# A graph network's prologue: one tied order for index look-up, one-hots and layer norm

## The chip, the cores and the metric

The kernel runs on one core of a Trainium2 chip. The metric is the device time of one execution in microseconds (us), the median of several runs on the same chip. Engines are named as in the profile: PE (TensorE, the matrix engine; PEld is its weight load), DVE (VectorE), ACT (ScalarE), POOL (GpSimd) and SP (SyncE). PE, DVE, ACT and POOL each work through their own instructions in the order in which the program lists them; semaphores tie them to each other.

## The reference

There are 6,250 nodes with 64 features and 206,250 directed edges (100,000 random pairs in both directions and a loop at each node), sorted by destination. Two residual layers follow each other:

```python
edge_index = jnp.stack([src, dst])
h = jnp.maximum(_layernorm(x, axis=-1), 0.0)
x = x + _L0_gnn_ref(h, edge_index, ...)   # two graph convolutions: sum over the edges, two dense layers each
h = jnp.maximum(_layernorm(x, axis=-1), 0.0)
x = x + _L1_gnn_ref(h, edge_index, ...)   # three dense layers per node, sum over the edges, three dense layers
```

All sums over edges use the same graph, so the kernel first turns the edge list into a matrix of edge counts and then multiplies by it.

## The kernel before

**Tiling.** The nodes are cut into 49 tiles of 128. The count matrix A is built tile by tile (index t): function `build` makes one-hot matrices on DVE (`there` L413, `high` L417, `low` L420), PE multiplies them into counts (L445; a block is 16 small products, and four blocks make a tile), and ACT copies each block out of PSUM into the tile `a` (L447). SP stores `a` to memory. While tile t is built, PE also does the first graph sum for tile t-1 (L588: 49 products with the normalized features `hp`), a quarter after each block. After the 49 tiles come two sweeps over the stored A (L754, L761), which this change does not touch.

**Index chain.** Tiles are handled in pairs; a batch b holds two pairs (batch 0 only one). For a batch, in this order: `search` (ACT L311 counts samples below a node; DVE L315 and L316 make a row number), `fetch_blocks` (POOL L324 gathers a block of 550 destinations per pair), `search_block` (ACT L335 counts in the block), `fetch_edges` (DVE L344 and L345 make offsets; POOL L349 gathers 128 windows of destinations and of sources, `d_win` and `s_win`), `slots` (eight kinds of DVE instruction, L372 to L388, that cut the indices into three fields), `cast` (ACT L394), `turn` (three PE transposes L402 into one bank, copied by ACT L404 into `lkw`), and then the one-hots. In the steady state each step of a later batch is put between the blocks of an earlier one, through the table `beside`, whose entries `between` runs after each block.

**Layer norm.** The features are normalized in seven chunks of seven tiles (XT = 7). `values(c)` calls `norm`: DVE mean (L238, L239), centred values `xm` (L241), ACT squares (L243), DVE sum of squares (L245), ACT root (L246), DVE reciprocal and scaling into `h` (L247, L248). Then `split` cuts `h` into three bf16 parts: ACT casts the first (L255), PE multiplies `h` by the identity and subtracts the parts already taken (L258, L260) into bank 0 and then bank 1 of a PSUM tile, and ACT copies each bank out (L261). The texts below call the L258 product into bank 0 the first product of a chunk and that into bank 1 the second. The PSUM pool `pcnt` has two tiles of two banks, shared by the splits and by the count blocks in program order. The tile `h` has two buffers, and so have the three one-hot tiles.

**Order.** The engine order comes from the tile framework's scheduler, except where `behind(op, other)` or `follow` adds a dependence without a semaphore between instructions of one engine. In the kernel before, the prologue's program order is: searches and block gathers of batches 0 and 1, `values` of chunks 0 and 1 around the gathers of batch 0, `slots` and `cast` of batch 0, gathers of batch 1, `turn` of batch 0, chunk 2, search of batch 2, chunk 3, search of batch 3, chunk 4, then the loop over tiles. Chunks 5 and 6 follow in the loop after tile 0's build. `slots`, `cast` and `turn` of batch 1 stand between the blocks of tile 0. The x chunks are loaded alternately from the SP queue (chunks 0, 2, 4, 6) and the ACT queue (1, 3, 5), behind the sample load `smp_i` on SP. Quoted with the function that the change rewrites most:

```python
    def values(t):
        h = work.tile([P, XT, D], FP, name="h")
        begun, centered, squared = norm(h, t, XT)
        if t <= XT:
            behind(begun, sampled)
            behind(begun, bounds)
            behind(squared, searched[0])
        if t == XT:
            behind(centered, searched[1])
        split(hp[:, t:t + XT], h)
```

Of the kernel before, what the change touches and what calls it, by code (L numbers as in the profile page):

```python
# [32 lines left out]
FP = mybir.dt.float32  # L33
I32 = mybir.dt.int32
I16 = mybir.dt.int16
# [5 lines left out]
OP = mybir.AluOpType  # L41
# [107 lines left out]
def load_x(nc, xs, x, engines):  # L149
    full = N // P  # L150
    nc.vector.memset(xs[:, full, :], 0.0)
    for i, t in enumerate(range(0, full, XT)):
        n = min(XT, full - t)
        engines[i % len(engines)].dma_start(xs[:, t:t + n, :], x[t * P:(t + n) * P].rearrange("(t p) d -> p t d", p=P))
    engines[0].dma_start(xs[:N - full * P, full, :], x[full * P:])


@with_exitstack
def fast(ctx: ExitStack, tc: tile.TileContext, x, src, dst, w, bad, out):
# [14 lines left out]
    def bank(name, dtype=FP):  # L174
        return pmix.tile([P, CH * 4 // mybir.dt.size(dtype)], dtype, tag="mix", name=name)


    root = const.tile([P, 1], FP, name="root")
    nc.scalar.activation(root, w.eps, AF.Sqrt)
# [1 line left out]
    with nc.allow_non_contiguous_dma(reason="samples"):  # L181
        nc.sync.dma_start(smp_i, dst.rearrange("(k c b) -> k c b", c=SP_COLS, b=BLK)[:, :, 0])
    xs = const.tile([P, NT, D], FP, name="xs")
    load_x(nc, xs, x, [nc.sync, nc.scalar])
    w.load(nc.sync)


# [9 lines left out]
    nc.vector.tensor_scalar(ident_a, w.ident, 1.0 / UNIT, None, op0=OP.mult)  # L197
# [9 lines left out]


    smp_f = once.tile([SP_ROWS, SP_COLS], FP, name="smp_f")
    nc.vector.tensor_copy(smp_f, smp_i)  # L210
    nc.vector.memset(smp_f[0:1, 0:1], -1.0)
    smp_d = once.tile([SP_ROWS, SP_COLS, SP_ROWS], FP, name="smp_d")
    shape = [SP_ROWS, SP_COLS, SP_ROWS]
# [20 lines left out]
    def norm(to, t, n):  # L234

        xt = xs[:, t:t + n, :]
        mean = work.tile([P, n], FP, name="mean", tag=f"mean{n}")
        begun = nc.vector.tensor_reduce(mean, xt, axis=AX.X, op=OP.add)  # L238
        nc.vector.tensor_scalar_mul(mean, mean, 1.0 / D)  # L239
        xm = work.tile([P, n, D], FP, name="xm", tag=f"xm{n}")  # L240
        centered = nc.vector.tensor_tensor(xm, xt, mean[:, :, None].to_broadcast([P, n, D]), op=OP.subtract)  # L241
        sq = work.tile([P, n, D], FP, name="sq", tag=f"sq{n}", bufs=1)
        squared = nc.scalar.activation(sq, xm, AF.Square)  # L243
        var = work.tile([P, n], FP, name="var", tag=f"var{n}")
        nc.vector.tensor_reduce(var, sq, axis=AX.X, op=OP.add)  # L245
        nc.scalar.activation(var, var, AF.Sqrt, bias=w.eps, scale=1.0 / D)  # L246
        nc.vector.reciprocal(var, var)  # L247
        nc.vector.scalar_tensor_tensor(to, xm, 0.0, var[:, :, None].to_broadcast([P, n, D]), op0=OP.max, op1=OP.mult)  # L248
        return begun, centered, squared

    def split(parts, h):

        parts = [parts[:, :, i * D:(i + 1) * D] for i in range(NP)]
        banks = pcnt.tile([P, 2, CH], FP, name="cnt")[:, :, :h.shape[1] * D]
        nc.scalar.copy(parts[0], h)  # L255
        for i in range(2):
            ps = banks[:, i].rearrange("p (t d) -> p t d", d=D)
            nc.tensor.matmul(ps, w.ident, h, start=True, stop=False)  # L258
            for k in range(i + 1):
                nc.tensor.matmul(ps, minus, parts[k], start=False, stop=(k == i))  # L260
            nc.scalar.copy(parts[i + 1], ps)  # L261
# [23 lines left out]
    counted, swept = {}, []  # L285

    def behind(op, other):

        tc.add_manual_dep(op.ins, other.ins.name,
                          mybir.DependencyInfo(mybir.DependencyClass.NoSync, mybir.DependencyReason.DATA),  # L290
                          reason="order on an engine")
        return op

    def follow(op, engine):

# [40 lines left out]
        follow(op, "ACT")  # L336
        return op

    def fetch_edges(b):

        if b >= len(BATCHES):
            return
        each, qs = tiles_of(b)
        nc.vector.scalar_tensor_tensor(off_f[:, qs], sign2[:, qs], -0.5, base[:, qs], op0=OP.mult, op1=OP.add)  # L344
# [10 lines left out]
    def slots(b):  # L355

        if b >= len(BATCHES):
            return
# [8 lines left out]

        def first(op):
            follow(op, "DVE")

        pair = temp("pair")
        first(nc.vector.tensor_scalar(pair, d, 1, PITCH // 2 - 1, op0=OP.logical_shift_right, op1=OP.bitwise_and))  # L372
# [2 lines left out]
        for i, q in enumerate(each):  # L375
# [12 lines left out]
        nc.vector.scalar_tensor_tensor(parts[:, :, 2, :].bitcast(I16), place, ONE_BITS, second,  # L388
                                       op0=OP.bitwise_or, op1=OP.bitwise_or)
        words[b] = word  # L390

    def cast(b):
# [3 lines left out]
    def turn(b, i):  # L396

        if b >= len(BATCHES):
            return
        ps = bank("ps_win", BF)  # L400
        for k in range(3):
            follow(nc.tensor.transpose(ps[:, k * P:(k + 1) * P], parts2[b % 2][:, i, k, :], identb), "PE")  # L402
        lkw = lkws[starts[b] + i] = wins.tile([P, 3, P], BF, name="lkw", bufs=5)
        nc.scalar.copy(lkw.rearrange("p a b -> p (a b)"), ps[:, :3 * P])  # L404

    def hot(lkw, g0, n):
# [6 lines left out]
        nc.vector.tensor_tensor(there, word2[:, None, :, :].to_broadcast(shape),  # L413
                                of(0)[:, :, None, :].to_broadcast(shape), op=OP.is_equal)
# [5 lines left out]
        counted["DVE"] = nc.vector.tensor_tensor(  # L420
            low.rearrange("p (g i) w -> p g i w", i=2), there.rearrange("p g w i -> p g i w"),
            of(2)[:, :, :, None].to_broadcast([P, n // 2, 2, W]), op=OP.mult)
        return low.bitcast(F8), high

    def store(t, a):
# [8 lines left out]
    def build(t, between):  # L434
# [1 line left out]
        a = amat.tile([P, H, G], I16, name="a", tag="a")  # L436
        lkw = lkws[t // 2]
        for g0, m in FIRST_HOTS if t == 0 else ((0, G),):
            low, high = hot(lkw, (t % 2) * G + g0, m)
            for k in range(g0, g0 + m, 2 * PG):  # L440
                ps = pcnt.tile([P, 2, CH], FP, name="cnt")
                for b in range(2):
# [68 lines left out]
    def values(t):  # L511
        h = work.tile([P, XT, D], FP, name="h")
        begun, centered, squared = norm(h, t, XT)
        if t <= XT:
            behind(begun, sampled)
            behind(begun, bounds)
            behind(squared, searched[0])
        if t == XT:
            behind(centered, searched[1])
        split(hp[:, t:t + XT], h)  # L520


    beside = {}
    for b in range(len(BATCHES)):
        step = BATCHES[b]

        def at(u, what, *args):
            beside.setdefault(8 * starts[b] + u * step // 2, []).append((what, args))

        at(0, slots, b + 1)  # L530
        at(4, cast, b + 1)
        for i in range(BATCHES[b + 1] if b + 1 < len(BATCHES) else 0):
            at(7 + 2 * i, turn, b + 1, i)
        if b > 0:
            at(6, search, b + 4)
            for i in range(BATCHES[b + 3] if b + 3 < len(BATCHES) else 0):
                at(10 + 2 * i, search_block, b + 3, i)
            at(13, fetch_edges, b + 3)
            at(14, fetch_blocks, b + 4)
# [10 lines left out]
    fetch_blocks(0)  # L550
    search(1)
    fetch_blocks(1)
    values(0)
    search_block(0, 0)
    fetch_edges(0)
    values(XT)
    slots(0)
    cast(0)
    for i in range(2):
        op = search_block(1, i)  # L560
    fetch_edges(1)
    turn(0, 0)
    values(2 * XT)
    search(2, op)
    fetch_blocks(2)
    values(3 * XT)
    search(3)
    fetch_blocks(3)
    values(4 * XT)
    for i in range(2):  # L570
        search_block(2, i)
    fetch_edges(2)

    r1, acc1 = {}, {}

# [31 lines left out]
    for t in range(NT + 1):  # L607
        last_total, total = total, FirstSum(t - 1, a) if t else None
        if t < NT:
# [7 lines left out]

            a = build(t, between)
            if t == 0:
                values(5 * XT)  # L620
                for i in range(2):
                    search_block(3, i)
                fetch_edges(3)
                values(6 * XT)
                search(4)
                fetch_blocks(4)
            if t == 1:
# [416 lines left out]
```

## Time and profile before

| what | value |
|---|---|
| median of 3 runs | 892.75 us (892.65 to 893.2) |
| profiled execution, its own time | 895.53 us |
| profiled execution, span of the trace | 893.7 us |
| busy in the span: PE, DVE, ACT, POOL | 96%, 71%, 63%, 14% |
| mean granted TensorE clock | 0.989 |
| PE busy from 61.1 to 120 us | 57.58 of 58.90 us |
| PE busy from 0 to 61.1 us | 38.46 of 61.10 us |

The span is what the trace covers; 1.8 us of the profiled execution lie around it. The last line adds the seven windows of the prologue (1.62 + 5.51 + 4.32 + 5.14 + 5.94 + 8.78 + 7.15). A timeline line gives the start in us, the time in us, engine, source line and operation, output and input, and the number of merged instructions; a bracket tells how long the engine was idle before it and who released it. Note that one product with fp32 operands is two instructions in the trace.

### The profile page before, as it was taken

How to read it: one execution, taken by the hardware profiler on the slowest of the kernel's cores; microseconds unless marked ns; L12 is line 12 of the kernel's file. 1: busy time of each engine (PE TensorE's matmuls, PEld its weight loads, DVE VectorE, ACT ScalarE, POOL GpSimd, SP SyncE). 2: the span in 40 equal slices, each digit the busy share in tenths (PEclk: the TensorE clock that was granted, in tenths of full speed). 3: DMA queues.
4: the chain of work that ended last, by engine and by line, in shares of the span. 5: the costliest groups of instructions: out<-in, count | busy, mean ns of one | idle time of the engine just before them, and what ended most of it. 6: DMA issues, size and time to landing. Idle time of an engine off the chain costs nothing.

```text
span 893.7 us, 19691 instructions
## 1 busy us (share of the span) xinstructions
PE 854.5 (96%) x8227; PEld 730.8 (82%) x8227; DVE 633.7 (71%) x908; ACT 566.0 (63%) x761; POOL 126.9 (14%) x86
## 2 busy tenths in 40 slices
PE   3789999999999999999999999999999999999996
PEld 1369999999999999978887878888889877777784
DVE  6889999999999999645545555554556676767662
ACT  5757776667776666645555555555546579777763
POOL 4535334354342200000000000000000000000000
PEclk9799999999999999999999999999999999999998
DMA  6335564455545534644444444444434677777771
GB/s 145 103 99 163 150 171 130 140 165 159 142 134 145 148 111 130 198 131 125 129 123 118 124 129 124 118 121 133 128 92 125 181 222 244 232 235 234 218 220 38
DMA packets 148326, 133.57 MB, mean 149 GB/s; under 512 B 29988, under 2 KB 110500, under 8 KB 148228
## 3 DMA queue, kind: packets, MB, share of 16 engines
q1 hardware_dynamic: 141784, 121.19, 46.5%
q0 software_dynamic: 3600, 10.32, 4.4%
q8 instruction: 66, 1.08, 0.5%
q10 hardware_dynamic: 2844, 0.72, 0.4%
q14 instruction: 32, 0.26, 0.1%
HBM read 91.25 MB, written 40.94 MB: 148 GB/s over the span
## 4 chain that ended last, share of the span: by engine, by line
PE 88%; ACT 4%; DMA 3%; DVE 2%; issue 2%; SPq 0%; POOL 0%; ACTq 0%; DVEq 0%
PE acc L761 43%; PE acc L588 23%; PE cnt L445 9%; PE ps_t L458 6%; PE ps_y L467 3%; ACT ar L754 2%; DMA a<-A 2%; PE ps_g L508 1%; PE cnt L258 1%; DMA xs<-in_x_dram 1%; ACT t L460 1%; ACT a L447 1%; PE acc L590 0%; DMA blk<-in_dst_dram,row 0%; PE ps_win L402 0%
## 5 line engine op out<-in xcount | busy, mean ns | idle before, releaser
L754 DVE CAST ar<-a 128x2048 fp32r<-128x2048 uint8 (+1 forms) x200 | 220.4, 1110 | 183.1 <-PE acc L761 158.4
L754 ACT CAST ar<-a 128x2048 fp32r<-128x2048 uint8 (+2 forms) x126 | 232.2, 1845 | 126.4 <-PE acc L761 108.6
L761 PE MATMUL acc<-ar,h2r 128*128 128x512 f32 (+2 forms) x1274 | 297.6, 388 | 0.0
L761 PEld LDWEIGHTS acc<-ar,h2r 128*128 128x128 f32 x1274 | 229.3, 188 | 49.8 <-issue 5.8
L588 PE MATMUL acc<-hp,a 128*128 128x193 bf16 x2401 | 237.1, 247 | 6.6 <-issue 5.8
L447 ACT ACTIVATE a<-cnt 128x784 int16<-128x784 f32 x196 | 160.8, 822 | 83.9 <-PE cnt L445 82.8
L588 PEld LDWEIGHTS <-a 128*128 128x128 fp8e4 x2401 | 196.4, 98 | 10.0 <-issue 7.8
L761 PE MATMUL acc<-ar,yr 128*128 128x512 f32 (+2 forms) x637 | 157.6, 399 | 0.0
L761 PEld LDWEIGHTS acc<-ar,yr 128*128 128x128 f32 x637 | 115.7, 188 | 32.5 <-issue 9.8
L445 PEld LDWEIGHTS <-low 128*128 128x128 fp8e4 x3136 | 107.6, 96 | 10.7 <-issue 10.4
L445 PE MATMUL cnt<-high,low 128*128 128x49 bf16 x3136 | 114.1, 186 | 1.8 <-ACT a L447 1.6
L420 DVE TENSOR_TENSOR low<-there,lkw 128x2048 int32<-128x2048 bf16 (+2 forms) x51 | 112.2, 2199 | 0.0
L417 DVE TENSOR_TENSOR high<-high,lkw 128x3136 bf16<-128x3136 bf16 (+2 forms) x51 | 87.9, 1723 | 19.5 <-PE cnt L445 18.7
L324 POOL DMA_INDIRECT blk<-in_dst_dram,row x25 | 48.0, 1918 | 99.3 <-DVE base L316 86.7
L413 DVE TENSOR_TENSOR there<-word,lkw 128x2048 bf16<-128x2048 bf16 (+2 forms) x51 | 59.1, 1177 | 0.9 <-ACT lkw L404 0.4
L349 POOL DMA_INDIRECT s_win<-in_src_dram,off x25 | 45.4, 1815 | 7.6 <-issue 7.6
L349 POOL DMA_INDIRECT d_win<-in_dst_dram,off x25 | 31.4, 1254 | 72.5 <-DVE off L345 64.9
L258 PE MATMUL cnt<-h,ident 128*128 128x448 f32 x28 | 19.6, 804 | 13.2 <-DVE h L248 9.1
L460 ACT ACTIVATE t<-ps_t,d 128x512 f32<-128x512 f32 (+2 forms) x26 | 17.3, 664 | 11.2 <-PE ps_t L458 11.1
L460 ACT ACTIVATE t<-ps_t,c 128x512 f32<-128x512 f32 (+1 forms) x26 | 17.1, 662 | 11.4 <-PE ps_t L458 11.4
L258 PEld LDWEIGHTS cnt<-h,ident 128*128 128x128 f32 x28 | 5.8, 252 | 19.6 <-issue 10.8
L335 ACT ACTIVATE junk<-blk,below_node 128x550 bf16<-128x550 int32 x25 | 18.7, 749 | 3.8 <-DMA blk<-in_dst_dram,row 3.8
(122 smaller groups left out, 598.2 us busy)
## 6 DMA issues: line engine op xcount, KB each, us to landing
a<-A SPq DMA_DIRECT2D x276, 256.0 KB
A<-a SPq DMA_DIRECT2D x49, 768.0 KB
a<-A SPq DMA_DIRECT2D x24, 192.0 KB
a<-A SPq DMA_DIRECT2D x22, 64.0 KB
out_dram<-o SPq DMA_DIRECT2D x11, 128.0 KB
A<-a SPq DMA_DIRECT2D x49, 16.0 KB
xs<-in_x_dram ACTq DMA_DIRECT2D x3, 224.0 KB
xs<-in_x_dram SPq DMA_DIRECT2D x3, 224.0 KB
```

Source lines behind the costliest of these rows:

```text
L324: nc.gpsimd.indirect_dma_start(out=blks[q], out_offset=None, in_=dst.rearrange("(r b) -> r b", b=BLK), in_offset=bass.IndirectOffsetOnAxis ...
L349: nc.gpsimd.indirect_dma_start(out=win[:, i, :], out_offset=None, in_=of.rearrange("(a o) -> a o", o=1), in_offset=bass.IndirectOffsetOnAx ...
L413: nc.vector.tensor_tensor(there, word2[:, None, :, :].to_broadcast(shape), of(0)[:, :, None, :].to_broadcast(shape), op=OP.is_equal)
L417: nc.vector.tensor_tensor(high, high2[:, None, :, :].to_broadcast(shape), of(1)[:, :, None, :].to_broadcast(shape), op=OP.is_equal)
L420: counted["DVE"] = nc.vector.tensor_tensor(low.rearrange("p (g i) w -> p g i w", i=2), there.rearrange("p g w i -> p g i w"), of(2)[:, :, ...
L445: counted["PE"] = nc.tensor.matmul(ps[:, b, j * H:(j + 1) * H], low[:, g, :], high[:, g // 2, :, g % 2], start=True, stop=True)
L447: counted["ACT"] = nc.scalar.activation(a[:, :, k:k + 2 * PG].rearrange("p h (b j) -> p h b j", b=2), ps[:, :, :PG * H].rearrange("p b (j ...
L458: placed(nc.tensor.matmul(ps[:, :n * P], wt, rhs, start=(i == 0), stop=(i == len(terms) - 1)))
L460: nc.scalar.activation(to, ps[:, :n * P], AF.Relu, bias=bias)
L588: nc.tensor.matmul(acc[:, t % 2, :], self.a[:, k, :], hp[:, k], start=(k == 0), stop=False)
L754: widen(ar.rearrange(f"p k t b -> {order}"), a.rearrange(f"p t (k b) -> {order}", b=P))
L761: op = nc.tensor.matmul(acc[:, :n * P], part, ar[:, k - k0].rearrange("p t b -> p (t b)"), start=(k == 0 and i == 0), stop=(k == H - 1 and ...
```

## The change

The arithmetic is the same; order and queues change.

- Loads: chunk 0 of x comes first on the ACT queue; chunks 0, 2, 4, 6 go there and 1, 3, 5 and the rest to SP.
- The convert of the samples (L210) is tied behind the four constants on DVE.
- `norm` also returns the sum of squares and the final scaling, so that they can be tied. `values` takes a chunk number and a tie for each of the five instructions that `norm` returns; `whole=False` leaves the split to a later `parts_of`.
- In `split` the first PE product is tied behind the last transpose and the last count product so far.
- `slots(0)` and the first `there` are tied behind chunk 3's `xm`; the offsets of batch 1 too. The second `there` of tile 0 is tied behind chunk 4's end, and chunk 4 begins behind the last instruction of `slots(0)`.
- Chunk 4 moves into tile 0 after its first block, `slots(1)` and `cast(1)` with chunk 5 after its last block, chunk 6 after tile 1's first block. The second transposition of batch 1 moves to the place of the first. Search and block gathers of batch 2 move ahead of chunk 3's split, those of batch 3 into tile 0.

```diff
-    engines[0].dma_start(xs[:N - full * P, full, :], x[full * P:])
+    engines[-1].dma_start(xs[:N - full * P, full, :], x[full * P:])
...
-    load_x(nc, xs, x, [nc.sync, nc.scalar])
+    load_x(nc, xs, x, [nc.scalar, nc.sync])
...
-    nc.vector.tensor_copy(smp_f, smp_i)
+    behind(behind(nc.vector.tensor_copy(smp_f, smp_i), constants), bounds)
...
-            nc.tensor.matmul(ps, w.ident, h, start=True, stop=False)
+            op = nc.tensor.matmul(ps, w.ident, h, start=True, stop=False)
+            for other in ("turn", "PE"):
+                if other in counted:
+                    behind(op, counted[other])
...
-            low, high = hot(lkw, (t % 2) * G + g0, m)
+            low, high = hot(lkw, (t % 2) * G + g0, m, {0: normed[3][1], 16: normed.get(4, [None])[-1]}.get(g0) if t == 0 else None)
...
+    def values(c, *others, whole=True):
+
+        h = hs[c] = work.tile([P, XT, D], FP, name="h")
+        normed[c] = norm(h, c * XT, XT)
+        for op, other in zip(normed[c], others):
+            if other:
+                behind(op, other)
+        if whole:
+            parts_of(c)
+
+    def parts_of(c):
+        split(hp[:, c * XT:(c + 1) * XT], hs.pop(c))
...
-        at(0, slots, b + 1)
-        at(4, cast, b + 1)
+        if b > 0:
+            at(0, slots, b + 1)
+        if b > 0:
+            at(4, cast, b + 1)
         for i in range(BATCHES[b + 1] if b + 1 < len(BATCHES) else 0):
-            at(7 + 2 * i, turn, b + 1, i)
+            at(7 + 2 * i if b else 7, turn, b + 1, i)
...
-    values(0)
+    values(0, sampled, None, searched[0])
+    values(1, searched[1])
     search_block(0, 0)
     fetch_edges(0)
-    values(XT)
-    slots(0)
-    cast(0)
+    values(2)
     for i in range(2):
         op = search_block(1, i)
-    fetch_edges(1)
+    values(3, normed[2][-1], whole=False)
+    fetch_edges(1, normed[3][1])
+    slots(0, normed[3][1])
+    cast(0)
     turn(0, 0)
-    values(2 * XT)
     search(2, op)
     fetch_blocks(2)
-    values(3 * XT)
-    search(3)
-    fetch_blocks(3)
-    values(4 * XT)
-    for i in range(2):
-        search_block(2, i)
-    fetch_edges(2)
+    parts_of(3)
+
+    def fourth():
+        normed[4] = None
+        values(4, counted["slots"], None, None, firsts[0])
+
+    def fifth():
+        slots(1, counted["DVE"])
+        cast(1)
+        values(5, counted["slots"])
+
+    def sixth():
+        values(6, counted["DVE"])
+
+    beside[0] = [(fourth, ()), (search, (3,)), (fetch_blocks, (3,))] + beside.get(0, [])
+    beside[3] = [(search_block, (2, 0)), (search_block, (2, 1)), (fetch_edges, (2,)), (fifth, ())] + beside.get(3, [])
+    beside[4] = [(sixth, ())] + beside.get(4, [])
...
             if t == 0:
-                values(5 * XT)
                 for i in range(2):
                     search_block(3, i)
                 fetch_edges(3)
-                values(6 * XT)
                 search(4)
                 fetch_blocks(4)
```

More of the change, by code (lines that the diff above doesn't have):

```diff
@@ L175, in bank, with behind @@
         return pmix.tile([P, CH * 4 // mybir.dt.size(dtype)], dtype, tag="mix", name=name)
+    def behind(op, other):
+        tc.add_manual_dep(op.ins, other.ins.name,
+                          mybir.DependencyInfo(mybir.DependencyClass.NoSync, mybir.DependencyReason.DATA),
+                          reason="order on an engine")
+        return op
     root = const.tile([P, 1], FP, name="root")
@@ L196, in fast @@
     ident_a = const.tile([P, P], BF, name="ident_a")
-    nc.vector.tensor_scalar(ident_a, w.ident, 1.0 / UNIT, None, op0=OP.mult)
+    constants = nc.vector.tensor_scalar(ident_a, w.ident, 1.0 / UNIT, None, op0=OP.mult)
     word2 = once.tile([P, W, 2], BF, name="word2")
@@ L244, in norm @@
         var = work.tile([P, n], FP, name="var", tag=f"var{n}")
[L245 removed]
+        summed = nc.vector.tensor_reduce(var, sq, axis=AX.X, op=OP.add)
         nc.scalar.activation(var, var, AF.Sqrt, bias=w.eps, scale=1.0 / D)
         nc.vector.reciprocal(var, var)
[L248 to L249 removed]
+        ended = nc.vector.scalar_tensor_tensor(to, xm, 0.0, var[:, :, None].to_broadcast([P, n, D]), op0=OP.max, op1=OP.mult)
+        return begun, centered, squared, summed, ended
     def split(parts, h):
@@ L283, in tiles_of @@
         return range(starts[b], starts[b] + BATCHES[b]), slice(starts[b], starts[b] + BATCHES[b])
[L285 to L292, printed above, removed]
+    counted, firsts, swept = {}, [], []
     def follow(op, engine):
@@ L337, in search_block, with fetch_edges @@
         return op
-    def fetch_edges(b):
+    def fetch_edges(b, before=None):
         if b >= len(BATCHES):
@@ L343, in fetch_edges @@
         each, qs = tiles_of(b)
-        nc.vector.scalar_tensor_tensor(off_f[:, qs], sign2[:, qs], -0.5, base[:, qs], op0=OP.mult, op1=OP.add)
+        op = nc.vector.scalar_tensor_tensor(off_f[:, qs], sign2[:, qs], -0.5, base[:, qs], op0=OP.mult, op1=OP.add)
+        if before:
+            behind(op, before)
         nc.vector.tensor_scalar(off[:, qs], off_f[:, qs], float(E - P), None, op0=OP.min)
@@ L353, in fast, with slots @@
     words = {}
-    def slots(b):
+    def slots(b, before=None):
         if b >= len(BATCHES):
@@ L369, in first @@
             follow(op, "DVE")
+            if before:
+                behind(op, before)
         pair = temp("pair")
@@ L387, in slots @@
         place, second = (t.bitcast(I16).rearrange("p q (a b) -> p q a b", b=2)[:, :, :, 0] for t in (place, second))
-        nc.vector.scalar_tensor_tensor(parts[:, :, 2, :].bitcast(I16), place, ONE_BITS, second,
-                                       op0=OP.bitwise_or, op1=OP.bitwise_or)
+        counted["slots"] = nc.vector.scalar_tensor_tensor(parts[:, :, 2, :].bitcast(I16), place, ONE_BITS, second,
+                                                          op0=OP.bitwise_or, op1=OP.bitwise_or)
         words[b] = word
@@ L401, in turn, with hot @@
         for k in range(3):
-            follow(nc.tensor.transpose(ps[:, k * P:(k + 1) * P], parts2[b % 2][:, i, k, :], identb), "PE")
+            op = nc.tensor.transpose(ps[:, k * P:(k + 1) * P], parts2[b % 2][:, i, k, :], identb)
+            follow(op, "PE")
+        counted["turn"] = op
         lkw = lkws[starts[b] + i] = wins.tile([P, 3, P], BF, name="lkw", bufs=5)
         nc.scalar.copy(lkw.rearrange("p a b -> p (a b)"), ps[:, :3 * P])
-    def hot(lkw, g0, n):
+    def hot(lkw, g0, n, before=None):
         def of(i):
@@ L412, in hot @@
         there = hots.tile([P, G // 2, W, 2], BF, name="there")[:, :n // 2]
-        nc.vector.tensor_tensor(there, word2[:, None, :, :].to_broadcast(shape),
-                                of(0)[:, :, None, :].to_broadcast(shape), op=OP.is_equal)
+        op = nc.vector.tensor_tensor(there, word2[:, None, :, :].to_broadcast(shape),
+                                     of(0)[:, :, None, :].to_broadcast(shape), op=OP.is_equal)
+        if before:
+            behind(op, before)
         shape = [P, n // 2, H, 2]
@@ L422, in hot @@
             of(2)[:, :, :, None].to_broadcast([P, n // 2, 2, W]), op=OP.mult)
+        firsts.append(counted["DVE"])
         return low.bitcast(F8), high
@@ L509, in third_product @@
         halves(h2r[:, t:t + n], ps[:, :n * HID].rearrange("p (t f) -> p t f", f=HID))
[L511 to L520, printed above, removed]
+    normed, hs = {}, {}
+    def values(c, *others, whole=True):
[8 more added lines that the diff above has]
+        split(hp[:, c * XT:(c + 1) * XT], hs.pop(c))
     beside = {}
```

## The prediction

> **What bounds the kernel.** I read the busy windows first, then the timelines of PE, DVE and ACT over the first 62 us, then the waits. Columns of the windows: PE, PEld, DVE, ACT, POOL busy, granted clock, DMA share, GB/s.
>
> ```profile
> 53.00:61.10 8.10, 7.15 (x125) 5.70 (x124) 6.23 (x17) 5.69 (x10) 3.31 (x3) 0.88 0.35 103
> 61.10:120.00 58.90, 57.58 (x1066) 56.62 (x1062) 57.39 (x68) 40.34 (x70) 22.90 (x12) 1.00 0.59 164
> ```
>
> From 61.1 us PE is busy without a break; DVE is nearly as full, but its one-hots are ready 1 us or more before PE takes them (`low` of tile 3 ends at 64.1, PE begins it at 65.10). So the change is worth what it moves one event: the start of the second count block of tile 2, from which PE runs through. I call it E; before it stands at 60.69. The rest of the kernel follows E one for one, since PE holds 88% of the chain. Before E:
>
> ```profile
> 25.42 1.74 PE L258 MATMUL cnt<-h,ident 128*128 128x448 f32 x4 [0.68 <-ACT lkw L404]
> ...
> 28.61 1.02 PE L258 MATMUL cnt<-h,ident 128*128 128x448 f32 x2 [0.87 <-ACT hp L261]
> ...
> 32.01 1.86 PE L258 MATMUL cnt<-h,ident 128*128 128x448 f32 x2 [1.99 <-DVE h L248]
> ...
> 51.23 1.56 PE L258 MATMUL cnt<-h,ident 128*128 128x448 f32 x2 [2.22 <-DVE h L248]
> ...
> 58.79 0.58 PE L445 MATMUL cnt<-high,low 128*128 128x49 bf16 x16
> 59.56 1.28 PE L588 MATMUL acc<-hp,a 128*128 128x193 bf16 x13 [0.20 <-ACT a L447]
> 60.69 0.58 PE L445 MATMUL cnt<-high,low 128*128 128x49 bf16 x16
> ```
>
> PE waits for `h` of the last chunks (51.23 is chunk 6), because the count blocks of tile 1 stand behind the splits of chunks 5 and 6 in the shared PSUM tiles. One product (two instructions) takes 0.87 us warm (25.42: two in 1.74) and 1.86 cold. The second product of a chunk starts when ACT has copied the first bank out (34.88 behind the copy of 34.28), so a split is a chain PE, ACT, PE, ACT.
>
> ```profile
> 9.95 0.14 DVE L315 TENSOR_SCALAR row<-sign 128x1 int32<-128x1 f32 x1
> ...
> 22.82 0.27 DVE L388 SCALAR_TENSOR_TENSOR parts<-place,second 128x128 int16<-128x128 int16 x1
> ...
> 26.66 0.69 DVE L420 TENSOR_TENSOR low<-there,lkw 128x512 int32<-128x512 bf16 x1
> ...
> 36.04 1.22 DVE L420 TENSOR_TENSOR low<-there,lkw 128x1024 int32<-128x1024 bf16 x1
> ...
> 41.10 0.62 DVE L248 SCALAR_TENSOR_TENSOR h<-xm,var 128x448 f32<-128x448 f32 x1
> ...
> 50.46 0.62 DVE L248 SCALAR_TENSOR_TENSOR h<-xm,var 128x448 f32<-128x448 f32 x1
> ```
>
> The last two are `h` of chunks 5 and 6. I now walk the changed order of each engine with the durations of these rows.
>
> **Head.** The samples still land at 5.10 (L210 starts there). Before, four constants ran behind them and the product `smp_d` began at 5.80; now they run at 1.4 to 2.0, as the identity is done at 1.38, so it begins at 5.40: -0.40. Chunk 0 is first on ACT's queue: by the DMA view that queue had moved 904 packets by 3.0 us, and a chunk has 896, so it is there; the wait to 7.30 goes. What is late next is ACT's count: its accumulator read ends at 9.26 - 0.40 = 8.86. Before, the row number waited further behind chunk 2's mean (9.95); now it follows at 8.89, -1.06. The gather is issued at 9.32 and lands 3.96 later, at 13.28 (10.38 to 14.34 before); the x load runs until about 9.5 in both, so I allow +0.5. ACT's fourth load waits for the sample load at 5.10, while ACT is idle until 7.65; SP's weights start one DMA earlier: both nothing. Offsets come at 14.37 (15.56 before), `d_win` lands at 18.7, `s_win` at 19.7: -1.2.
>
> **Slots of batch 0.** Here the gain is lost. They are tied behind chunk 3's `xm`, its mean behind chunk 2's `h`. That `h` needs the buffer of chunk 0, free when PE has done chunk 0's second product. This waits for ACT's copy, which queues behind the block count of batch 1: gather issued 11.2, landing 4.68 later as before (12.09 to 16.77) at 15.9, then 0.65, 0.45 and 0.5 on ACT to 17.5, then 1.86 cold on PE: 19.4. So `h` of chunk 2 runs at 19.45 (not 18.05, when its reciprocal is ready), the mean at 20.0, row numbers 20.6, `xm` 20.9 to 21.5. The windows have lain there for 1.8 us. The slots are 1.53 us of DVE, with offsets (0.17) and a sum of squares (0.52) between: end at 23.77, against 23.09. The transposes follow at once (23.8 instead of 24.22, where splits stood ahead), `lkw` is ready at 24.6, chunk 3's `h` takes 24.5 to 25.05, and the first `low` ends at 26.6 instead of 27.35: -0.75.
>
> **Tile 0.** DVE: `xm` of chunk 4 and `high` to 27.6; the third `high` needs PE's first block done, 28.8 (16 products with chunk 3's second product between: 0.35 + 0.9 + 0.4 + 0.35), so 28.85; reciprocal 29.95; `h` of chunk 4 30.1 to 30.7; two `there` 1.0; row numbers, released by ACT at 31.25; two `low` 0.6 + 1.2: last at 33.6, -3.6. The slots of batch 1, which before lay in front of it, are 2.3 us. PE: chunk 4's first product starts at 30.75 after 1.95 us of idleness, nearest the row at 32.01: cold, 1.86. Then copy 33.4, second product and subtraction 2.6 (34.88 to 37.48), copy 36.6; this frees the PSUM tile for the third block. Evictions at 0.72 each follow one another: last one 38.05 to 38.8, against 40.75 to 41.58: -2.8.
>
> **The price.** ACT counts in the blocks of batch 2 only then: 0.66, cast 0.3, 0.76, read: 40.65. DVE stands at the offsets of batch 2 from 39.0 (33.55 + slots 2.3 + `there` 1.13 + `high` 1.7 + gaps 0.3) and loses 1.7 us; behind them wait chunk 5's mean and `low` of tile 1, now 41.4 to 43.6 (before 43.33 to 45.62). Then DVE runs, by its order: `xm` of chunk 5 0.6, mean of chunk 6 0.6, small ones 0.4, `there` 1.13, sum of squares 0.6, `high` 1.7, `xm` 0.7, `h` of chunk 5: ends 49.85 (before 41.72). `low` of tile 2 2.2, sum of squares 0.55, half of batch 2's slots 1.4, `h` of chunk 6: ends 54.6 (before 51.08). PE finishes what it has of tile 0's graph sum (35 of 49 products) at 41.5 and is idle for 8.4 us, since its order has chunk 5's first product ahead of tile 1's blocks. From 49.9, cold for 3.4 us as from 51.5 to 54.9 before: first product 1.86, subtraction 0.4, 13 counts 0.55, second product 1.4 and subtractions 0.5, copy to 55.1; chunk 6: product 0.9, eviction and counts to 56.6, copy 57.1, product 0.9, subtractions 0.4, copy 58.95; blocks three and four to 59.85; 8 sums and an eviction, tile 2's first block 60.6; 0.4, 13 sums 1.1: **E at 62.1, +1.4 us**.
>
> Other queues: POOL now has two block gathers (2.5 us) in front of batch 1's windows, which land at 30.7 and are used at 33.6: hidden by 2.9 us of one-hots. Batch 2's windows start at 41.65, take 7.0 us for four like those from 47.06 to 54.1 before, land at 51.2 and are used from 52.6: 1.4 us of cover. Tile 0's store starts earlier: nothing. Weights in two pieces before tile 3 stay behind tile 1's evictions, 2 us before PE's need.
>
> [...] The row shows 1.86 after 1.99 us. [...]
>
> **Rivals.** [...] (2) The lead carries: tile 0 is out 2.8 us earlier, and if chunks 5 and 6 keep up, E keeps that: 889.9. For it: PE's largest waits before are for `h`. Against: DVE has 24 us of listed work between 28.85 and chunk 6's `h`. (3) Late windows, on the slow side: if each gather of batch 2 is issued under a one-hot at 2.43 us (the row at 51.66), they land at 54.8, 2 us after the slots want them, and chunk 6's `h` and E go with them: +3.4, 896.2; it decides once four issues take over 8.4 us. A late first gather has the same place with 0.5. (4) The change does not do what it says: partly so, the slots of batch 0 come no earlier.
>
> **Numbers.** The sum is made against the profiled span, 893.7 (895.53 with what lies around it). +1.4 on the median of the runs, 892.75, gives 894.2. What can be told from no change is 0.2%, 1.8 us. Forecast 0.43 (893.3 to 895.4; a third of it over 1.8), warm 0.22 (891.4 to 893.3), lead carries 0.14 (888.9 to 891.2), late windows or waits that add up 0.21 (895.2 to 897.5). Faster 0.15, within 0.2% 0.47, slower 0.38. The range 890.9 to 897.0 leaves out most of the lead and the end of the last case.
>
> **What would show it.** Row number near 8.9 and first `low` ending near 26.6; last slot instruction of batch 0 after 23; a DVE wait for ACT of 1 to 2 us near 39 to 41; PE idle for over 6 us before chunk 5's first product near 50; `h` of chunk 6 near 54.6. I am wrong if chunk 5's `h` comes before 47, or the second block of tile 2 stands before 59 or after 64.

## The result and the profile after

The changed kernel takes 896.31 us (median of 6 runs, 895.62 to 897.79) where the kernel before takes 892.70 (6 runs, 892.58 to 893.20): a ratio of 1.0040, 95% interval 1.0027 to 1.0054. It is 3.6 us slower. The time lies inside the range of the prediction, but 0.9 us above its forecast case (893.3 to 895.4), in the stretch that it had kept for late windows. The side it fell on, slower by more than 0.2%, had a chance of 0.38, and no change 0.47.

The profiled execution of the changed kernel took 895.69 us (span 893.8), 0.6 under its median. The busy windows of it, with the columns of the windows shown before (PE, PEld, DVE, ACT, POOL, granted clock, DMA share, GB/s):

```profile
42.00:53.00 11.00, 3.56 (x19) 1.91 (x18) 11.00 (x22) 4.45 (x12) 9.48 (x6) 0.69 0.12 33
53.00:61.10 8.10, 6.62 (x86) 4.17 (x85) 5.36 (x12) 4.71 (x8) 5.28 (x5) 1.00 0.32 104
61.10:120.00 58.90, 57.45 (x1085) 56.71 (x1082) 55.95 (x68) 40.87 (x72) 22.90 (x12) 1.00 0.57 158
```

The loss shows in the first line. DVE has no free moment from 42 to 53 us and PE works for 3.56 of 11 us; before, PE had worked for 8.78 us there. From 61.1 on the two kernels are alike (57.45 and 57.58 us of 58.90). The timeline of PE in the changed kernel says what it waits for:

```profile
31.39 0.99 PE L265 MATMUL cnt<-h,ident 128*128 128x448 f32 x2 [3.00 <-DVE h L255]
...
33.23 1.86 PE L265 MATMUL cnt<-h,ident 128*128 128x448 f32 x2
...
49.51 1.83 PE L265 MATMUL cnt<-h,ident 128*128 128x448 f32 x2 [7.34 <-DVE h L255]
...
54.64 1.02 PE L265 MATMUL cnt<-h,ident 128*128 128x448 f32 x2 [0.55 <-DVE h L255]
...
61.60 1.28 PE L618 MATMUL acc<-hp,a 128*128 128x193 bf16 x13
62.73 0.58 PE L457 MATMUL cnt<-high,low 128*128 128x49 bf16 x16
```

The products at 49.51 and 54.64 are the first ones of chunks 5 and 6. The long wait of 7.34 us is for `h` of chunk 5, and the last line is E, the second count block of tile 2: 62.73. The timeline of DVE in the same execution shows why `h` is late:

```profile
8.84 0.16 DVE L318 TENSOR_SCALAR row<-sign 128x1 int32<-128x1 f32 x1 [1.55 <-ACT junk L314]
...
23.19 0.29 DVE L395 SCALAR_TENSOR_TENSOR parts<-place,second 128x128 int16<-128x128 int16 x1
...
25.58 0.68 DVE L431 TENSOR_TENSOR low<-there,lkw 128x512 int32<-128x512 bf16 x1
...
40.42 0.16 DVE L347 SCALAR_TENSOR_TENSOR off_f<-sign,base 128x2 f32<-128x2 f32 x1 [1.31 <-ACT junk L338]
...
44.71 1.22 DVE L422 TENSOR_TENSOR there<-word,lkw 128x2048 bf16<-128x2048 bf16 x1
...
46.45 1.78 DVE L428 TENSOR_TENSOR high<-high,lkw 128x3136 bf16<-128x3136 bf16 x1
...
48.75 0.62 DVE L255 SCALAR_TENSOR_TENSOR h<-xm,var 128x448 f32<-128x448 f32 x1
49.28 2.28 DVE L431 TENSOR_TENSOR low<-there,lkw 128x2048 int32<-128x2048 bf16 x1
...
53.60 0.62 DVE L255 SCALAR_TENSOR_TENSOR h<-xm,var 128x448 f32<-128x448 f32 x1
```

The head is quicker (row number 8.84 instead of 9.95) and tile 0's first one-hot ends at 26.26. But `there` and `high` of tile 2 (44.71 and 46.45) stand ahead of `h` of chunk 5, and its `low` (49.28) ahead of `h` of chunk 6. PE takes tile 2 from 60.88 on, and takes chunk 5 first. DVE makes first what PE wants last. In the kernel before, `h` of chunk 5 (41.10) stood ahead even of tile 1's `high`, and `h` of chunk 6 (50.46) behind tile 2's `there` and `high`.

### The profile page after: what moved, and what is told of

The parts are those of the page before. It is cut to its first block, busy times and chain, and to the rows that moved or that the text cites. A ratio compares the mean times of both kernels' runs of the same rounds, so it can differ in the third digit from the quotient of the medians.

```text
span 893.8 us, 19688 instructions
## 1 busy us (share of the span) xinstructions
PE 851.0 (95%) x8227; PEld 729.5 (82%) x8227; DVE 634.5 (71%) x908; ACT 566.4 (63%) x761; POOL 129.4 (14%) x86
## 4 chain that ended last, share of the span: by engine, by line
PE 89%; DVE 3%; ACT 2%; DMA 2%; issue 2%; SPq 0%; ACTq 0%; DVEq 0%
PE acc L789 45%; PE acc L618 22%; PE cnt L457 9%; PE ps_t L470 6%; PE ps_y L479 3%; DMA a<-A 1%; PE ps_g L520 1%; PE cnt L265 1%; DVE ar L782 1%; ACT ar L782 1%; DMA smp_i<-in_dst_dram 0%; ACT t L472 0%; PE acc L620 0%; PE ps_win L409 0%; DVE h L255 0%
## 5 line engine op out<-in xcount | busy, mean ns | idle before, releaser
L327 POOL DMA_INDIRECT blk<-in_dst_dram,row x25 | 49.9, 1998 | 105.2 <-DVE base L319 97.5
L422 DVE TENSOR_TENSOR there<-word,lkw 128x2048 bf16<-128x2048 bf16 (+2 forms) x51 | 59.1, 1178 | 0.4
```

The costliest lines, as they stand in the source:

```text
L327: nc.gpsimd.indirect_dma_start(out=blks[q], out_offset=None, in_=dst.rearrange("(r b) -> r b", b=BLK), in_offset=bass.IndirectOffsetOnAxis ...
L422: op = nc.vector.tensor_tensor(there, word2[:, None, :, :].to_broadcast(shape), of(0)[:, :, None, :].to_broadcast(shape), op=OP.is_equal)
```

## Experiments

The first theory, **late order**, is this reading: the layer norms of chunks 5 and 6 come behind tile 2's one-hots, and tie order on DVE is the loss. Its rivals were the DVE stall on the counts of batch 2 (the 1.31 us at 40.42), the slots of batch 0 held back by their new tie to chunk 3's `xm` (the expectations call these two **early ties**), and the head; later, the **clock**: that PE's products turn slow (1.83 instead of 0.9 to 1.0 us, with the granted clock at 0.50 instead of 1.00) behind the long idle stretch. Slow products are also called cold, fast ones warm.

These runs fell in four sessions, each with its own runs of the kernel before. Its median was 884.08, 884.35 and 883.09 us in three of them and 892.40 in the fourth, so only ratios within a session compare kernels (a ratio can differ a little from the quotient of the two medians). The changed kernel has two readings, 1.0040 in the session of the result and 1.0058 here, with overlapping intervals; what an edit takes back is counted below from 1.0058, which was measured at the level of the edits, and is 1.6 us less from 1.0040. E is from one profiled execution each, whose own time stands beside it.

| kernel | median, us | before, us | ratio, 95% interval | profiled: own time, E |
|---|---|---|---|---|
| before again | 884.72 | 884.08 | 0.9999 (0.9983 to 1.0014) | 884.60, 58.25 |
| after again | 889.49 | 884.35 | 1.0058 (1.0036 to 1.0080) | 889.49, 63.79 |
| norm before tile 2 | 885.63 | 884.08 | 1.0020 (1.0009 to 1.0031) | 887.76, 58.85 |
| counts early | 888.95 | 884.08 | 1.0053 (1.0034 to 1.0071) | 888.51, 62.62 |
| slots untied | 886.17 | 884.08 | 1.0025 (1.0015 to 1.0036) | 889.26, 60.91 |
| head alone | 883.70 | 884.35 | 0.9993 (0.9977 to 1.0009) | 880.66, 56.16 |
| untied, norm before tile 2 | 884.21 | 884.35 | 1.0003 (0.9985 to 1.0021) | 885.28, 58.53 |
| untied, norm before tile 1 | 881.42 | 884.35 | 0.9964 (0.9952 to 0.9977) | 880.47 |
| after, filled | 885.17 | 883.09 | 1.0014 (0.9999 to 1.0028) | 885.26, 60.13 |
| before, filled | 879.87 | 883.09 | 0.9957 (0.9944 to 0.9970) | 882.12, 54.67 |
| after, order only | 895.34 | 892.40 | 1.0029 (1.0020 to 1.0038) | 892.68, 60.37 |
| before, filled, same order | 892.18 | 892.40 | 0.9998 (0.9989 to 1.0008) | 889.55, 57.39 |

**Both kernels again.**

> The kernel before, unchanged, for a second profile. The first profiled execution took 895.53 us while the runs had a median of 892.7. If the difference lay in the prologue, the second block of tile 2 starts at about 58 instead of 60.69 and the stretch from there to the end takes 833.0 us again; if it lay behind the prologue, that block starts near 60.7 again and the stretch to the end takes about 830 to 831 us, as it does in the changed kernel (831.1).

> The changed kernel, unchanged, on the chip of this call. If the first result holds elsewhere, it is 3 to 5 us slower than the kernel before, and the second block of tile 2 starts at 62 to 63.

The second profiles of the two kernels are both close to their medians. The timeline of PE of the kernel before, second execution:

```profile
31.71 1.02 PE L258 MATMUL cnt<-h,ident 128*128 128x448 f32 x2 [1.91 <-DVE h L248]
...
49.45 0.99 PE L258 MATMUL cnt<-h,ident 128*128 128x448 f32 x2 [1.98 <-DVE h L248]
...
58.25 0.58 PE L445 MATMUL cnt<-high,low 128*128 128x49 bf16 x16
```

and of the changed kernel, second execution:

```profile
49.38 1.83 PE L265 MATMUL cnt<-h,ident 128*128 128x448 f32 x2 [7.35 <-DVE h L255]
...
55.46 1.86 PE L265 MATMUL cnt<-h,ident 128*128 128x448 f32 x2 [0.51 <-ACT hp L271]
...
63.79 0.58 PE L457 MATMUL cnt<-high,low 128*128 128x49 bf16 x16
```

In the kernel before, the first products of chunks 4 and 6 run at 1.0 us here and E is 58.25, not 60.69 with 1.86 at 32.01. That fits a difference in the prologue, but the stretch from E to the end is 824.6 us, which neither case of the expectation had: the rest of the kernel is quicker here, too. In the changed kernel the idle stretch came again (7.35 after 7.34 us), and this time chunk 6's first product (55.46) was slow as well. From these two profiles E moved by 5.5 us, where it had moved by 2.0 in the first pair.

**Norm before tile 2.** Chunk 6's last instruction is put ahead of tile 2's first two one-hot instructions.

```diff
-  .get(g0) if t == 0 else None)
+  .get(g0) if t == 0 else normed[6][-1] if t == 2 else None)
...
-        nc.vector.tensor_tensor(high, ...)
+        op = nc.vector.tensor_tensor(high, ...)
+        if before and n == G:
+            behind(op, before)
```

> The changed kernel, with the one-hots of tile 2 tied behind the end of chunk 6's layer norm. Theory late order (the loss is that chunks 5 and 6 stand behind tile 2's one-hots on DVE): h of chunk 5 ends at 46.8 instead of 49.4, h of chunk 6 at 48.3 instead of 54.2, the second block of tile 2 starts at 59.1 instead of 62.73, time 892.5 to 893.5. Theory early ties (the loss is made before tile 1, by the slots of batch 0 and the block counts of batch 2): at most 0.7 us is gained, about 895.7.

DVE and PE of this kernel:

```profile
45.29 0.63 DVE L255 SCALAR_TENSOR_TENSOR h<-xm,var 128x448 f32<-128x448 f32 x1
47.06 0.62 DVE L255 SCALAR_TENSOR_TENSOR h<-xm,var 128x448 f32<-128x448 f32 x1
47.61 1.22 DVE L422 TENSOR_TENSOR there<-word,lkw 128x2048 bf16<-128x2048 bf16 x1
```
```profile
46.06 1.83 PE L265 MATMUL cnt<-h,ident 128*128 128x448 f32 x2 [4.88 <-DVE h L255]
...
58.85 0.58 PE L459 MATMUL cnt<-high,low 128*128 128x49 bf16 x16
```

`h` of chunk 6 comes 6.5 us earlier than in the changed kernel and PE's wait falls to 4.88 us; the product is still slow, and E is 58.85, close to the 59.1 that late order gave. The kernel is 1.6 us behind before where the changed one is 5.1 behind: late order carries a large part, by itself and with the clock left cold.

**Counts early.** The block counts of batch 2 move to the first block of tile 0, ahead of the evictions they had waited behind.

```diff
-    beside[0] = [(fourth, ()), (search, (3,)), ...
-    beside[3] = [(search_block, (2, 0)), (search_block, (2, 1)), (fetch_edges, (2,)), ...
+    beside[0] = [(fourth, ()), (search_block, (2, 0)), (search_block, (2, 1)), (search, (3,)), ...
+    beside[3] = [(fetch_edges, (2,)), ...
```

> The changed kernel, with the two block counts of batch 2 on ACT moved from behind tile 0's last eviction to its first. Theory late order: the DVE wait of 1.3 us at 39.1 goes, everything behind it moves up by 1.0 to 1.3 us, time about 895.2, still slower than before. Theory early ties with this wait as its main part: 2 us or more, no slower than before.

```profile
41.28 0.16 DVE L347 SCALAR_TENSOR_TENSOR off_f<-sign,base 128x2 f32<-128x2 f32 x1 [1.57 <-ACT junk L338]
```

The stall did not go: the offsets of batch 2 came at 33.42 without a wait, but the timeline of DVE has 1.57 us at 41.28, now at the offsets of batch 3, whose count on ACT waits for its block's DMA in turn (0.45 us ahead of 40.40). Ratio 1.0053, no gain. One wait has taken the place of another, and what a DVE without it would bring was not seen.

**Slots untied.** The offsets of batch 1 and the slots of batch 0 lose their tie to chunk 3.

```diff
-    fetch_edges(1, normed[3][1])
-    slots(0, normed[3][1])
+    fetch_edges(1)
+    slots(0)
```

> The changed kernel without the two ties to chunk 3's centred values, so that the slots of batch 0 and the offsets of batch 1 run as soon as their data are there. Theory late order: the slots of batch 0 end 2 to 3 us earlier, the first one-hots 0.5 to 1.5 us earlier, and 0 to 1.5 us of it reach the second block of tile 2; the time stays above 894.5. Theory early ties: 2.5 us or more are gained, time 893.8 or less.

The timelines of DVE and PE:

```profile
21.44 0.28 DVE L395 SCALAR_TENSOR_TENSOR parts<-place,second 128x128 int16<-128x128 int16 x1
```
```profile
31.39 1.02 PE L265 MATMUL cnt<-h,ident 128*128 128x448 f32 x2 [0.30 <-ACT hp L271]
...
46.45 1.83 PE L265 MATMUL cnt<-h,ident 128*128 128x448 f32 x2 [7.73 <-DVE h L255]
...
60.91 0.58 PE L457 MATMUL cnt<-high,low 128*128 128x49 bf16 x16
```

The slots end at 21.72 instead of 23.48 and the product of chunk 5 begins 3.1 us earlier; PE's idle stretch stays (7.73), it only lies earlier. Part of that is the clock: chunk 4's second product (31.39) took 1.02 us, where it had taken 1.86 (33.23) in the changed kernel. The kernel is 2.1 us behind before. The tie cost some 3 us of the 5.1, more than late order left for it: it is a second cause beside the late order, and not a step of it.

**Untied, with norm before tile 2** is the last two edits together.

> The changed kernel with both of the edits that helped: the slots of batch 0 untied, and chunks 5 and 6 normalized before the one-hots of tile 2. Theory late order: the gains add, h of chunk 5 ends near 43 and h of chunk 6 near 44.5, the second block of tile 2 starts at 56 to 57, time 1 to 2.5 us below the kernel before. If the two gains overlap, it stays where the second alone was, 1.5 us above the kernel before.

Nothing is left of the loss that can be told from no change (1.0003, 0.9985 to 1.0021). Each alone took back about 3 us, and together they take back 5: they shorten one chain and do not add up in full.

**Head alone.** The kernel before with the new order of the x loads and the samples' convert behind the constants.

```diff
-    load_x(nc, xs, x, [nc.sync, nc.scalar])
+    load_x(nc, xs, x, [nc.scalar, nc.sync])
...
-    nc.vector.tensor_copy(smp_f, smp_i)
+    behind(behind(nc.vector.tensor_copy(smp_f, smp_i), constants), bounds)
```

> The kernel before with only the head of the change: x loads alternating from the ACT queue first, and the convert of the samples behind the four constants. Theory late order: the first row number comes 1 us earlier, the time moves by -1.2 to 0.3 us, not slower. Rival (the new load order delays a later chunk or the weights): slower by 0.5 us or more, with a DVE wait for an x chunk.

0.9993 with 1 inside the interval: no change that can be told. Its one profile, E 56.16, is of an execution 3.0 us under the median (880.66 for 883.70), a warning against reading E off one profile.

**Untied, with norm before tile 1.** Chunks 5 and 6 are both normalized right behind tile 0's last one-hot, and tile 1's first one-hots wait for them.

```diff
     def fifth():
+        values(5, counted["DVE"])
+        values(6, counted["DVE"])
         slots(1, counted["DVE"])
         cast(1)
-        values(5, counted["slots"])
...
-    beside[4] = [(sixth, ())] + beside.get(4, [])
...
-  .get(g0) if t == 0 else normed[6][-1] if t == 2 else None)
+  .get(g0) if t == 0 else normed[6][-1] if t == 1 else None)
```

> As the last, but chunks 5 and 6 are normalized before the one-hots of tile 1, so that PE splits them while DVE makes these one-hots. Theory late order: PE's idle stretch before chunk 5's product goes, the second block of tile 2 follows the one-hots of tile 2 by about 2 us and starts near 53, time 3 to 5 us below the kernel before. Rival (the prologue is bound by DVE's total work, so the order of the norms does not matter): 0.5 us at most against the last.

The last line is shown against the version with norm before tile 2. PE of this kernel:

```profile
39.57 0.99 PE L265 MATMUL cnt<-h,ident 128*128 128x448 f32 x2
...
41.39 1.02 PE L265 MATMUL cnt<-h,ident 128*128 128x448 f32 x2 [0.46 <-ACT hp L271]
...
52.06 1.00 PE L459 MATMUL cnt<-high,low 128*128 128x49 bf16 x32
...
59.52 1.01 PE L459 MATMUL cnt<-high,low 128*128 128x49 bf16 x32 [0.61 <-DVE low L433]
```

The wait before chunk 5 is gone, the products of chunks 5 and 6 all run at 1.0 us, and the kernel beats both: 0.9964. The second block of tile 2 lies in the 32 products from 52.06 on, near the 53 that was expected. PE then waits for tile 3's `low` (59.52), so DVE is the next limit, and E no longer marks the point from which PE runs through. In this profile the clock stays at 1.00 from 24 us on, so what order and clock gained here is not told apart.

**After, filled.** The order on DVE stays late, but PE is kept busy: 76 products with unused results between the last transposes of batch 1 and chunk 5's product.

```diff
-        values(5, counted["slots"])
+        values(5, counted["slots"], whole=False)
+    def filled():
+        ps = bank("ps_fill")
+        for k in range(76):
+            op = nc.tensor.matmul(ps[:, :HP], identb, hp[:, k % 28], start=True, stop=True)
+            behind(behind(op, counted["turn"]), counted["PE"])
+        counted["turn"] = op
+        parts_of(5)
...
+    beside[3] = ... + [(filled, ())]
```

> The changed kernel, with 76 products (hp with the identity, 193 columns, about 0.1 us each, their results unused) put on PE between the last transposes of batch 1 and chunk 5's first product, where it was idle for 7.3 us. One eviction (tile 1's first) also moves ahead of a square root on ACT. If the loss is the wait for chunk 5's and 6's h (late order), the clock is only a follower: chunk 5's first product still starts at 49.5, takes 0.9 instead of 1.83, E comes at 62.0 to 62.8 (63.8 in the last run of the changed kernel, 62.73 in the first), and the ratio falls from 1.0058 to 1.003 to 1.005. If the cold clock after the long idle stretch is the loss itself, E falls by 3 us or more, to 60 or below, and the ratio is at most 1.002.

PE:

```profile
41.07 6.67 PE L600 MATMUL ps_fill<-hp,identb 128*128 128x193 bf16 x76
47.57 0.93 PE L626 MATMUL acc<-hp,a 128*128 128x193 bf16 x9
49.10 1.02 PE L265 MATMUL cnt<-h,ident 128*128 128x448 f32 x2 [0.59 <-DVE h L255]
...
60.13 0.58 PE L457 MATMUL cnt<-high,low 128*128 128x49 bf16 x16
```

`h` of chunk 5 ends at 49.04, no more than 0.3 us earlier than in the changed kernel, and yet E falls to 60.13 and the ratio to 1.0014 (0.9999 to 1.0028), about what was expected if the slow clock is itself the loss, and below the 1.003 to 1.005 of a clock that only follows. But the fillers also moved the order that the scheduler gives PE: all 16 counts of tile 1's first block now stand ahead of chunk 5's second product, where 13 had.

**After, order only** gives the changed kernel that order by ties, without fillers.

```diff
+            seconds.append(op)
...
+                if t == 1 and k in (0, 16):
+                    behind(seconds[11 if k == 0 else 13], counted["PE"])
```

> The changed kernel with PE's order around chunks 5 and 6 as the fillers had brought it (all 16 products of tile 1's first block ahead of chunk 5's second product, the same for the second block and chunk 6), but with no fillers: PE stays idle for 7.3 us before chunk 5. If the fillers had worked by the clock, nothing is gained here: chunk 5's products cold at 1.83, E 62.7 to 64.5, ratio 1.004 to 1.007. If their gain came from the order, E is 60 to 61 and the ratio 1.001 to 1.0025.

```profile
31.01 0.99 PE L267 MATMUL cnt<-h,ident 128*128 128x448 f32 x2 [2.93 <-DVE h L255]
...
32.82 1.02 PE L267 MATMUL cnt<-h,ident 128*128 128x448 f32 x2
...
47.91 1.83 PE L267 MATMUL cnt<-h,ident 128*128 128x448 f32 x2 [7.34 <-DVE h L255]
...
60.37 0.57 PE L460 MATMUL cnt<-high,low 128*128 128x49 bf16 x16
```

The ratio, 1.0029 (1.0020 to 1.0038), is between what the two theories gave, and its interval reaches only into that of the order. It was run where the kernel before stood at 892.40, close to the 892.70 of the result, for which the changed kernel had 1.0040 (1.0027 to 1.0054): the order alone is worth 0 to 2 us there, and the intervals overlap. Its E of 60.37 is of its quickest execution (892.68; median 895.34) and says little: chunk 5's product began 1.6 us earlier, of which 0.4 stood already at chunk 4's first product (31.01 for 31.39) and most of the rest came with chunk 4's second one (32.82), which happened to be warm. Counted from the start of chunk 5's first product to E, it took 12.46 us with the clock at half for 5.9 of them. "Counts early", with the old order on PE here, took 12.92 with 5.5 at half, and "after, filled" 11.03 with none. By these single profiles the order is worth about 0.5 us and the clock about 1.4. A filler that leaves the order alone was not run on the changed kernel, so the split stays an estimate.

**Before, filled.** 20 fillers in each of the two gaps of 2 us ahead of the first products of chunks 4 and 6.

```diff
+            if i == 0 and fill:
+                spare = bank("ps_fill")
+                for k in range(fill):
+                    last = behind(nc.tensor.matmul(spare[:, :HP], identb, hp[:, k % 21], start=True, stop=True), counted["split"])
...
-        split(hp[:, t:t + XT], h)
+        split(hp[:, t:t + XT], h, {4 * XT: 20, 6 * XT: 20}.get(t, 0))
```

> The kernel before, with 20 such products ahead of chunk 4's first product (idle for 2.0 us) and 20 ahead of chunk 6's (idle for 2.0 us). If the clock in those two gaps is what decides where the kernel before lands between 881 and 889 us (E 56.2 in a run with warm products from 40 us on, 58.3 and 60.7 in others), its runs draw together near their lower end: median 881 to 882.5, ratio 0.996 to 0.998, E 55 to 56.5. If the clock does not matter, ratio 0.999 to 1.002 and the same spread.

0.9957, the best ratio of all, as the clock would have it. But here too the order moved: `h` of chunk 5 and a reduction changed places with neighbours on DVE, and PE's order changed around it. With 14 fillers in each gap it does not:

> The kernel before with 14 fillers (1.24 us) in each of the two gaps, the order of every other instruction on PE, DVE and ACT unchanged. If the last gain was the clock: most of it comes again, ratio 0.996 to 0.998, E 55 to 57, runs within some 4 us of each other. If it came from the order that the 20 fillers had brought along (a product and transposes ahead on PE, h of chunk 5 earlier on DVE): ratio 0.999 to 1.001 and the spread of before.

```profile
32.15 1.02 PE L262 MATMUL cnt<-h,ident 128*128 128x448 f32 x2 [0.79 <-issue]
...
40.42 1.75 PE L262 MATMUL cnt<-h,ident 128*128 128x448 f32 x2
...
49.26 0.99 PE L262 MATMUL cnt<-h,ident 128*128 128x448 f32 x2 [1.03 <-DVE h L248]
```

The products behind the fillers are warm in its profile, and nothing is gained: 0.9998, with runs from 889.55 to 895.17 beside 889.44 to 895.89 of before. So the clock in these two gaps is not what spreads the runs of the kernel before, and the gain with 20 fillers most likely came with the new order. This is not shown to the end: the 20 were run where the kernel before stood at 883.09 us and the 14 where it stood at 892.40, and the new order was not run without fillers. What spreads the runs stays open.

## Why the prediction was right and wrong

Its walk through the changed kernel held almost to the end (measured: the first profile):

| step | predicted | measured |
|---|---|---|
| row number | 8.89 | 8.84 |
| gather of batch 0 lands | 13.28 | 13.08 |
| slots of batch 0 end | 23.77 | 23.48 |
| first `low` of tile 0 ends | 26.6 | 26.26 |
| last `low` of tile 0 ends | 33.6 | 34.06 |
| last eviction of tile 0 ends | 38.8 | 38.62 |
| DVE's wait for ACT's count | 1.7 | 1.31 |
| `low` of tile 1 | 41.4 to 43.6 | 41.10 to 43.38 |
| `h` of chunk 5 ends | 49.85 | 49.37 |
| PE idle before chunk 5's product | 8.4 | 7.34 |
| `h` of chunk 6 ends | 54.6 | 54.22 |
| E | 62.1 | 62.73 |

**Head, slots, tile 0.** The lead of tile 0 was there, 3.0 us at its last eviction in the first pair of profiles (38.62 for 41.58), and was given back where the prediction said. In the second pair it was 1.4 us (38.48 for 39.86): about half of the lead that the prediction reckoned with belonged to the one execution that it read, whose clock was slow for longer (see below). That the head alone is worth nothing measurable fits its small gain. The clause "here the gain is lost" of the slots was right, and the untied run gives its price, some 3 us counted from 1.0058 and 1.3 from 1.0040, where the text gave none of its own.

**The price.** Its mechanism was right: chunks 5 and 6 come late on DVE, PE idles, because their splits stand ahead of tile 1's blocks. The two runs with the norms moved ahead show it. The wait on batch 2's counts, which the prediction made a link of this chain, was real but could not be taken out on its own.

**The mis-sized term: "E at 62.1, +1.4 us", then "+1.4 on the median of the runs".** The end of the shift was nearly right (62.73) and its start was not typical. 60.69 was read from an execution of 895.53 us, 2.8 over the median of its kernel. In that execution PE's clock stood at half from 31.0 to 37.9 us, in the second profile only from 33.4 to 36.8, and PE's first product of tile 0's graph sum began at 41.64 instead of 39.92. The second profile, close to its median in time (884.60 for 884.08), has E at 58.25, and the changed kernel's at its median 63.79: +5.5 instead of +1.4. The time moved by 5.1 us there and by 3.6 in the session of the result. Had the sum been kept against its own profile, 895.53 + 1.4 = 896.9, it would have come within 0.6 us of the result, though partly by luck: E was 0.6 later than forecast and the rest of that execution 1.9 shorter. The gap of 2.8 us stood in the table of times before, and no case took it up.

**"The row shows 1.86 after 1.99 us."** Chunk 4's first product was forecast from this row; it took 0.99 us (31.39), and the traces show where the clock stood. In the two first profiles the granted clock from 24 to 70 us is 1.00 or 0.50, and within each its changes lie whole multiples of 3.41 us apart, counted from 31.0 us before and from 32.4 after. The windows of the two profiles, cut in such steps, around chunk 4:

| profile | step ends at, us | PE busy in the step | clock in it | clock after it |
|---|---|---|---|---|
| before | 31.0 | 45% | 1.00 | 0.50 |
| before | 34.4 | 71% | 0.50 | 0.50 |
| before | 37.9 | 100% | 0.50 | 1.00 |
| after | 29.0 | 74% | 1.00 | 1.00 |
| after | 32.4 | 30% | 1.00 | 0.50 |
| after | 35.8 | 89% | 0.50 | 1.00 |

So the product at 32.01 of the row ran at the 0.50 that stood from 31.0 on, behind a step in which PE was busy for 45%, the last 1.0 us of it idle. In the second profile of the same kernel the clock fell at 33.4 (0.97 granted from 24 to 34 us), and the same product (31.71) took 1.02 us after nearly the same idle stretch (1.91). In the changed kernel chunk 4's first product (31.39) took 0.99 after 3.00 us of idleness, and its second one (33.23) 1.86, behind the fall at 32.4. For the later steps of the walk the miss made little: `low` of tile 1 came within 0.3 us of the text.

**"PE holds 88% of the chain, the rest follows E one for one."** Not in the first pair of profiles: E moved by 2.0 us and the span by 0.1, since from E to the end took 833.0 us before and 831.1 after. In the second pair it was 824.6 and 823.8: of 5.5 us, 0.7 were given back. Why the tail is shorter stays open.

**The rivals.** The lead did not carry: `h` of chunks 5 and 6 did not keep up. Late windows did not happen: DVE is busy for all of 42 to 53 us, with no wait for a window. That its 896.2 is within 0.1 us of the result is luck. That the change partly does not do what it says, the slots of batch 0 no earlier than before (23.48 for 23.09), was so. For the 891.4 to 893.3 us of warm no run of the changed kernel shows the term: chunk 4's two products both at 1.0 us came in neither of its profiles, where the second took 1.86. They came in the profile of "after, order only" (0.99 and 1.02), with chunk 5's product at 47.91 instead of 49.51 and E at 60.37; there the order on PE had changed too.

## What to carry to other kernels

Before a sum is added to a median, compare the profiled execution's own time with that median, and if they differ by more than the effect looked for, find out which row of the profile makes the difference or make the sum against the profile. When chunks of work are given new places on one engine, order them by when the next engine's program takes them: here PE took chunk 5, chunk 6, tile 1, tile 2, and making tile 2 before the chunks on DVE cost some 3 us, while making both chunks before tile 1, with the slots untied, beat the kernel before by 0.36%. Whether a product on PE will be slow cannot be read from one idle stretch of one profile: the same stretch gave 1.86 us in one execution and 1.02 in the next. A filler or a tie tried as a test can reorder the schedule around it, so compare the order in the two traces before a gain is put down to what was meant.

## What the runs showed of the hardware

**The clock changed in steps.** In the first profiles of the two kernels the granted clock from 24 to 70 us is 1.00 or 0.50, and its 10 changes lie whole multiples of 3.41 us apart within each: at 31.0, 37.9, 41.3, 44.7, 51.5 and 54.9 us before, at 32.4, 35.8, 46.1 and 52.9 after. In the second profile of the kernel before they lie at 33.4, 36.8, 40.2, 43.6, 50.5 and 53.9 (0.97 granted from 24 to 34 us, 0.71 to 42, 0.81 to 53 and 0.95 to 61.1). Cut in steps of 3.41 us, the two first profiles have five at full clock that ended with a fall, with PE busy for 0, 30, 35, 45 and 51%, and none of those with 61% or more did. At half clock the five that ended with a rise had PE busy for 89, 89, 96, 100 and 100%, and the two that did not for 0 and 71%. These shares are of this kernel's mix of products, with ends of products that are modelled.

**The same kernel has two levels of time:** 892.4 to 892.7 us in two sessions, 883.1 to 884.4 in three. The record gives one chip number, 14, to a session at 884.08 and to the one at 892.40. The levels do not come from the prologue: between 120 and 300 us, with the clock granted in full, PE was busy for 175.91 us in the first profile of the kernel before and for 179.81 in the second. The missing 4 us are pauses ahead of the graph sum's products (L588: 4.1 us idle in all against 0.2), for which the trace shows nothing that PE waits for. In the sessions of repeated runs the time also spread over 6 to 9 us from run to run, where the first six runs lay within 0.6. The cause of both stays open.
